# Restart zeros of a segmented scan: written by copies, or by the decays' own exponential

## The chip, the core and the metric

The kernel runs on one core of a Trainium2 chip. The metric is the device time of one execution in microseconds. The core's engines are TensorE (PE; its weight loads are PEld), VectorE (DVE), ScalarE (ACT), GpSimd (POOL) and SyncE (SP), which issues the DMAs. Each engine works through its own queue in order, and semaphores tie the queues together. "L815" is line 815 of the kernel before.

## What is computed

The input is an image batch of 8 x 256 x 48 x 48. Layer 0 is a group norm, a projection, a similarity of all 2304 tokens with each other, the 16 nearest per token, and a weighted mean of their features. Layer 1 is a group norm and two Mamba blocks in a row. What matters here is the recurrence in a Mamba block, over the tokens of an image, for each of 512 channels and 16 states:

```
dA = exp(dt[t] * A)              # A = -exp(A_log), negative
h  = h * dA + dt[t] * B[t] * x[t]
y[t] = sum over states of h * C[t]
```

A token's state is the decayed state of the token before it, plus an input. At the first token h is zero; later chunks of tokens go on from the chunk before.

## The kernel before

**Tiling.** The 2304 tokens are cut into 6 chunks of T = 384. One chunk of one block of one image is a *unit*; 8 images, 6 chunks and 2 blocks make 96 units. A unit has 16 *steps*, each with 32 channels; the 128 partitions hold those 32 channels four times, for four groups of states, so that each partition has Q = 4 states. A step falls into two *parts* of HQ = 2 states. That makes 3072 parts, and the main loop runs over them, with part m as its counter.

**A part.** `decay(m)` (L815) has ScalarE compute two rows of 384 exponentials, one for each state, from the replicated step sizes `dtr` with the decay rate as scale. They go to one of two PSUM tiles, used in turn (`decays(m)`). `make_bx` (L791) has GpSimd multiply the inputs, 4 states at a time, into `bx`. `run_scan(m)` (L830) has VectorE run one scan over both states at once, 2 x 385 elements: each state has a column ahead of its 384 tokens. In that *restart column* the decay is zero and `bx` holds the incoming state (`take_up`, L803 and L805), so the scan drops what it carried from the other state and begins from there.

**Who multiplies by C.** A table, `SHARE`, divides the parts. In 2040 parts the scan writes over `bx`, and GpSimd does the multiply (L860). In the other 1032 parts, here called *V parts*, the scan writes over the decays in PSUM, and VectorE does the multiply (L832). Afterwards the restart columns hold states in place of zeros, and since the decays' rows are only written from their second column on, ScalarE has to put the zeros back: in `carry(m)` L847 saves the last column's states for the next chunk (`h_st`; not needed in an image's last chunk), then L848 copies two zeros from a constant tile.

**Order.** It is written out by hand. Within a turn m of the loop ScalarE's queue gets `carry(m - 1)`, then `decay(m + 1)`, which writes the same PSUM tile that part m - 1 has left. VectorE's queue gets the scan of part m, with its multiply if it is a V part. Two tables, `between` and `behind`, place all other work of a unit (projections, convolution taps, normalization, loads) at fixed parts, ahead of the scan or behind it; layer 0 of the next image is spread over the same loop.

**Loads.** `load_rep` (L565) brings a step's 32 rows of step sizes (`dtr`) and of their products with x (`dtxr`) from HBM to four groups of partitions, as four DMAs of 48 KB, about every second part, into three buffers in turn.

Of the kernel before, what the change touches and what calls it, by code (L numbers as in the profile page):

```python
# [8 lines left out]
F32 = mybir.dt.float32  # L9
BF16 = mybir.dt.bfloat16  # L10
AF = mybir.ActivationFunctionType
ALU = mybir.AluOpType
# [3 lines left out]
P = 128  # L16
GSIZE = 8
TAKEN = -4.0
TINY = 1e-24
FAR = 64.0  # L20


@with_exitstack
def tile_conv_preact(
# [18 lines left out]
    nc = tc.nc  # L43
# [8 lines left out]
    T = 384  # L52
# [3 lines left out]
    G = 32  # L56
    J = P // G
    Q = NS // J
    HQ = 2
    H = DC - 1  # L60
    PARTS = Q // HQ
    STEPS = DI // G
# [6 lines left out]


    SHARE = ("GGVGGGVVGGGGGGVG", "GGGVGVVGVVVGVGVG", "VGVGVGVVGGVVGGVG")
    JR = 1
    assert N % T == 0 and N % P == 0 and T % P == 0 and NS % (J * HQ) == 0

    const = ctx.enter_context(tc.tile_pool(name="const", bufs=1))
# [12 lines left out]
    minus = const.tile([P, P], BF16, tag="minus", name="minus")  # L88
    nc.vector.tensor_scalar(minus, ident, -FAR, None, ALU.mult)
    three = const.tile([P, 1], F32, tag="three", name="three")  # L90
    nc.gpsimd.memset(three, 3.0)
    tiny = const.tile([P, 2], F32, tag="tiny", name="tiny")
    nc.gpsimd.memset(tiny[:, 0:1], -TINY)
    nc.gpsimd.memset(tiny[:, 1:2], TINY)
    ones_mean = const.tile([P, P], F32, tag="ones_mean", name="ones_mean")
# [38 lines left out]
    A_sb = const.tile([P, DEPTH, STEPS, Q], F32, tag="A_sb", name="A_sb")  # L134
# [15 lines left out]
                A_log[d].rearrange("(i g) s -> g i s", g=G)[:, :, j * Q : (j + 1) * Q],  # L150
            )
    nc.scalar.activation(A_sb, A_sb, AF.Exp)
    nc.vector.tensor_scalar(A_sb, A_sb, -1.0, None, ALU.mult)

    h_st = const.tile([P, DEPTH, STEPS, Q], F32, tag="h_st", name="h_st")
    tail = const.tile([P, DEPTH, CB, H], F32, tag="tail", name="tail")
# [1 line left out]
    def rsqrt_start(r, var, eps):  # L158

        nc.scalar.activation(r, var, AF.Ln, bias=eps)  # L160
        nc.scalar.activation(r, r, AF.Exp, scale=-0.5)

    def rsqrt_end(eng, r, var, eps, name):

        t = small.tile(list(r.shape), F32, tag="newton", name=f"nt_{name}")
        if eng is nc.gpsimd:
            v = small.tile(list(r.shape), F32, tag="newton_v", name=f"nv_{name}")
            eng.tensor_scalar(v, var, eps, -0.5, ALU.add, ALU.mult)
            eng.tensor_mul(t, r, r)
            eng.tensor_mul(t, t, v)  # L170
            eng.tensor_scalar(t, t, 1.5, None, ALU.add)
            eng.tensor_mul(r, r, t)
            return

        nc.scalar.activation(t, r, AF.Square)
        eng.scalar_tensor_tensor(var, var, eps, t, ALU.add, ALU.mult)
        eng.tensor_scalar(var, var, -0.5, 1.5, ALU.mult, ALU.add)
        eng.tensor_mul(r, var, r)
# [49 lines left out]
    def layer0(b, left, pool, ps0, alone):  # L228
# [50 lines left out]
        def inverse_norm(c):  # L279
            rn[c] = small.tile([P, TB], F32, tag="rn", name=f"rn_{b}_{c}")  # L280
            rsqrt_start(rn[c], n2[c], tiny[:, 1:2])
            rsqrt_end(nc.gpsimd, rn[c], n2[c], TINY, f"rn_{b}_{c}")

# [233 lines left out]
    with tc.tile_pool(name="first", bufs=1) as pool0, tc.tile_pool(  # L517
        name="first_ps", bufs=1, space=PSUM
# [7 lines left out]
    with tc.tile_pool(name="setup", bufs=2) as setup:  # L526
        for d in range(DEPTH):
            for t in range(DC, DC + 1):
                dg = setup.tile([P, DB, P], F32, tag="dg", name=f"dg_{d}_{t}")
                for k in range(DB):  # L530
                    f = cw[:, d, k, t : t + 1] if t < DC else dpar[:, d, k : k + 1]
# [3 lines left out]
    keep = ctx.enter_context(tc.tile_pool(name="keep", bufs=2))  # L535
# [2 lines left out]

    banks = [ps.tile([P, 1024], F32, tag=f"da{i}", name=f"da_{i}", bufs=1) for i in range(2)]
    for bank in banks:
        nc.vector.memset(bank, 0.0)

    zeros = const.tile([P, HQ], F32, tag="zeros", name="zeros")
    nc.gpsimd.memset(zeros, 0.0)

    def decays(m):
        return banks[m % 2][:, 511 - T : 513 + T]
# [8 lines left out]

    def load_rep(unit, what, ik):

        k, i0 = divmod(ik * JR, J)
        t = keep.tile([P, JR, T], F32, tag=f"{what}r", name=f"{what}r_{unit['u']}_{ik}", bufs=3)
        src = unit[f"{what}_d"][k].rearrange("(i g) t -> g i t", g=G)
        for j in range(J):
            nc.sync.dma_start(t[j * G : (j + 1) * G], src[:, i0 : i0 + JR, :])  # L565
        unit[f"{what}r"][ik] = t

    def load_bc(unit, i):
# [184 lines left out]
    def silu_z(unit):  # L753
# [3 lines left out]
        for e in range(DB - 1):  # L757
# [9 lines left out]
    units = [  # L767
        dict(at=order.index((c, d)), b=b, c=c, d=d, u=f"{b}_{c}_{d}", left=lefts[b], pe={}, xc={}, BC=[], z={}, pw={},
             dt=[], dt_d={}, dtx_d={}, dtr={}, dtxr={}, bx={}, y={}, inw={}, dmat={}, taps={}, xi={}, cv={},
             pd={})  # L770
        for b in range(B) for c, d in order
    ]
    NSTEP = len(units) * STEPS

    def at(n):

        return units[n // STEPS], n % STEPS, n % STEPS // J

    def on_pool(unit, i, p):

        stage = 2 if unit["b"] + 1 == B else 0 if TOPK[0] <= unit["at"] < TOPK[1] else 1
        return SHARE[stage][(i * PARTS + p) % BLOCK] == "G"

    def make_bx(n):


        if n >= NSTEP:
            return
        unit, i, k = at(n)
        bx = keep.tile([P, Q, 1 + T], F32, tag="bx", name=f"bx_{n}", bufs=8)  # L790
        nc.gpsimd.tensor_tensor(  # L791
            bx[:, :, 1:], unit["BC"][0],
            unit["dtxr"][i // JR][:, i % JR : i % JR + 1, :].to_broadcast([P, Q, T]), ALU.mult,
        )
        unit["bx"][i] = bx

    def take_up(n):

        if n >= NSTEP:
            return  # L800
# [6 lines left out]
    def decay(m):  # L807

        n, p = divmod(m, PARTS)
        if n >= NSTEP:  # L810
            return
        unit, i, k = at(n)
        da = decays(m)
        for s in range(HQ):
            nc.scalar.activation(  # L815
                da[:, s * (1 + T) + 1 : (s + 1) * (1 + T)], unit["dtr"][i // JR][:, i % JR, :],
                AF.Exp, scale=A_sb[:, unit["d"], i, p * HQ + s : p * HQ + s + 1],
            )

    def run_scan(m):  # L820
        n, p = divmod(m, PARTS)
        if n >= NSTEP:
            return
# [12 lines left out]

    def carry(m):


        n, p = divmod(m, PARTS)  # L840
        if not 0 <= n < NSTEP:
            return
        unit, i, k = at(n)
        if not on_pool(unit, i, p):
            h = decays(m).rearrange("p (q t) -> p q t", q=HQ)
            if unit["c"] + 1 < NCH:
                nc.scalar.copy(h_st[:, unit["d"], i, p * HQ : (p + 1) * HQ], h[:, :, T])  # L847
            nc.scalar.copy(h[:, :, 0], zeros)  # L848

    def pool_part(n):  # L850

        if not 0 <= n < NSTEP:
            return
# [47 lines left out]
    def leave(unit, cb):  # L901
# [17 lines left out]
        (-35, center), (7, in_proj, 5), (24, sum_states, 2), (-33, variance), (-21, in_proj, 0),  # L919
        (-15, taps, 1), (38, out_proj, 0), (-15, taps, 2), (-14, taps, 3), (-34, square),  # L920
        (39, leave, 0), (23, load_rep, "dt", 14), (5, load_rep, "dt", 5), (-4, load_bc, 1), (38, out_proj, 1),
        (17, load_d, 2), (-17, tap, 1), (18, load_rep, "dtx", 13), (-8, times_x, 1), (19, gate, 1),
        (-22, normal), (1, load_rep, "dt", 3), (0, load_rep, "dtx", 4), (15, load_rep, "dt", 10), (6, load_rep, "dtx", 7),
        (10, load_rep, "dtx", 9), (12, load_rep, "dtx", 10), (20, load_rep, "dtx", 14), (11, gate, 0), (-29, spread_root),
        (-19, load_in, 5), (33, load_out), (-22, load_in, 0), (21, load_rep, "dt", 13), (-20, tap, 0),
# [28 lines left out]
    for n in range(LEAD):  # L954
        make_bx(n)
    take_up(0)
    decay(0)
    other = iter(())
    begun, started = None, False
    end = max(part for part, *_ in between + behind)  # L960
    for m in range(PARTS * NSTEP - HOOKS + end + 1):
        n, p = divmod(m, PARTS)
        w, hook = divmod(m, HOOKS)
        if m % (HOOKS * len(order)) == 0:
            image = w // len(order) + 1
            other = layer0(image, lefts[image], keep, ps, False) if image < B else iter(())
            begun, started = None, False
        carry(m - 1)
        decay(m + 1)
        if p == 0:  # L970
            make_bx(n + LEAD)
            pool_part(n - 1)
            take_up(n + 1)
        else:
            carry_pool(n - 1)
        for f, unit, args in inner.get(m, ()):
            if f is load_v and unit["left"] is not units[w]["left"]:
                for _ in other:
                    pass
            f(unit, *args)  # L980
        run_scan(m)
        for f, unit, args in outer.get(m, ()):
            f(unit, *args)
        if not started:
            for _ in range(2):
                if begun is None:
                    begun = next(other, 0)
            started = begun is not None and (m + 1 - PHASE - begun) % BLOCK == 0
        else:
            next(other, None)  # L990
# [41 lines left out]
```

## Time and profile before

| | |
|---|---|
| time, median of 3 runs | 10088.27 us (10084.85 to 10095.08) |
| span of the profiled execution | 10083.0 us |
| layer 0 of the first image, alone | about the first 500 us |
| exponentials of the decays, L815 | 6144, mean 584 ns |
| scans, L830 | 2040 at 1747 ns into `bx`, 1032 at 1755 ns into `da` |
| multiply of a V part, L832 | 1032, mean 958 ns |
| save of the state, L847 | 832, mean 158 ns |
| zero copy, L848 | 1032, mean 163 ns, 168.0 us in all |
| loads of step sizes, `dtr` | 6144 of 48 KB, 1.8 us to landing in the median |

Each row is from the groups of instructions by line, or from the list of DMA issues. A group's busy time is no measure of what it costs: an engine that is ahead can do it while it would otherwise wait. The idle time ahead of a group and the name of who ended it tell where an engine is held up, and the chain of waits, followed back from the last instruction, tells which of these hold-ups passed to the end of the run.

### The profile page before, as it was taken

How to read it: one execution, taken by the hardware profiler on the slowest of the kernel's cores; microseconds unless marked ns; L12 is line 12 of the kernel's file. 1: busy time of each engine (PE TensorE's matmuls, PEld its weight loads, DVE VectorE, ACT ScalarE, POOL GpSimd, SP SyncE). 2: the span in 40 equal slices, each digit the busy share in tenths (PEclk: the TensorE clock that was granted, in tenths of full speed). 3: DMA queues.
4: the chain of work that ended last, by engine and by line, in shares of the span. 5: the costliest groups of instructions: out<-in, count | busy, mean ns of one | idle time of the engine just before them, and what ended most of it. 6: DMA issues, size and time to landing. Idle time of an engine off the chain costs nothing. (4 is left out here: it accounts for less than half of the span.)

```text
span 10083.0 us, 134837 instructions
## 1 busy us (share of the span) xinstructions
PE 8011.2 (79%) x36736; PEld 4387.2 (44%) x36736; DVE 8971.1 (89%) x7992; ACT 7487.2 (74%) x16998; POOL 8944.0 (89%) x3928
## 2 busy tenths in 40 slices
PE   8878886888868888688876888778886888866655
PEld 6544443444434444344443444344443444422222
DVE  4479998899979999799997999989998899988898
ACT  4477786778767777678776777777876778777776
POOL 0079998899989999799997999989998899999998
PEclk9989997899978999799988999889997899977777
DMA  1144444444444444444444444444445444444444
GB/s 31 34 126 122 137 128 144 118 133 124 140 132 130 124 137 129 135 125 137 124 140 128 128 129 135 131 132 126 135 127 146 119 131 128 137 133 133 140 137 121
DMA packets 1243512, 1271.44 MB, mean 126 GB/s; under 512 B 266592, under 2 KB 1215840, under 8 KB 1242752
## 3 DMA queue, kind: packets, MB, share of 16 engines
q1 hardware_dynamic: 1230496, 1262.45, 43.8%
q8 instruction: 293, 4.80, 0.2%
q14 instruction: 467, 3.83, 0.1%
q10 hardware_dynamic: 12256, 0.36, 0.1%
HBM read 1048.94 MB, written 212.86 MB: 125 GB/s over the span
## 5 line engine op out<-in xcount | busy, mean ns | idle before, releaser
L791 POOL TENSOR_TENSOR bx<-BC,dtxr 128x1536 f32<-128x1536 f32 x1536 | 5301.9, 3455 | 81.4 <-PE y L878 37.8
L815 ACT ACTIVATE da<-dtr,A_sb 128x384 f32<-128x384 f32 x6144 | 3585.8, 584 | 817.3 <-DVE bx L830 626.6
L830 DVE TENSOR_TENSOR_SCAN bx<-da,bx 128x770 f32<-128x770 f32 x2040 | 3525.2, 1747 | 191.8 <-ACT da L815 142.3
L860 POOL TENSOR_TENSOR bx<-bx,BC 128x1536 f32<-128x1536 f32 (+1 forms) x1320 | 3306.5, 2505 | 253.2 <-DVE bx L830 235.7
L830 DVE TENSOR_TENSOR_SCAN da<-da,bx 128x770 f32<-128x770 f32 x1032 | 1810.9, 1755 | 247.0 <-ACT da L815 161.8
L591 PE MATMUL pe<-vn,inw 128*128 128x384 f32 (+1 forms) x3072 | 1244.9, 539 | 406.9 <-DVE xr L913 89.9
L391 PE MATMUL psim<-pos 128*128 128x512 f32 (+1 forms) x2880 | 1377.8, 611 | 203.0 <-ACT sim L400 88.5
L457 PE MATMUL po<-feat,aT 128*128 128x256 f32 x5184 | 1358.1, 411 | 21.2 <-ACT aT L446 14.9
L878 PE MATMUL y<-bx,sel 128*32 128x384 f32 x12288 | 1232.3, 537 | 40.3 <-POOL bx L860 30.6
L457 PEld LDWEIGHTS po<-feat,aT 128*128 128x128 f32 x5184 | 1027.3, 205 | 367.0 <-issue 112.1
L832 DVE TENSOR_TENSOR bx<-da,BC 128x768 f32<-128x768 f32 x1032 | 989.1, 958 | 35.5
L591 PEld LDWEIGHTS pe<-vn,inw 128*128 128x128 f32 x3072 | 585.7, 205 | 924.0 <-issue 212.1
L391 PEld LDWEIGHTS psim<-pos 128*128 128x128 f32 x2880 | 553.4, 206 | 837.9 <-issue 464.3
L878 PEld LDWEIGHTS y<-bx,sel 128*32 128x32 f32 x12288 | 398.1, 119 | 862.7 <-issue 735.5
L691 DVE SCALAR_TENSOR_TENSOR xc<-pe,cw,xc 128x384 f32<-128x384 f32 x1152 | 696.3, 611 | 37.6 <-ACT xc L683 10.4
L721 PE MATMUL pd<-dbl,dtp_sb 16*128 16x384 f32 x768 | 417.5, 658 | 340.9 <-ACT dt L730 171.2
L847 ACT COPY h_st<-da 128x2 f32<-128x2 f32 x832 | 131.6, 158 | 589.7 <-DVE bx L832 582.7
L437 PE MATMUL pt<-ident,sim 128*128 128x128 f32 x2592 | 533.3, 288 | 43.0 <-DVE v L655 18.5
L446 ACT ACTIVATE aT<-pt 128x512 f32<-128x512 f32 (+1 forms) x720 | 387.6, 547 | 230.1 <-PE pt L438 225.8
L896 PE MATMUL pw<-z,ow 128*128 128x384 f32 x1536 | 529.5, 497 | 21.0 <-DVE v L655 7.4
L429 ACT ACTIVATE rest<-left,three 128x512 bf16<-128x512 f32 (+1 forms) x720 | 467.0, 670 | 59.8 <-DVE left L414 59.8
L875 PE MATMUL y<-xc,dmat 128*128 128x384 f32 x768 | 391.7, 597 | 148.8 <-DVE xc L691 124.6
(148 smaller groups left out, 10057.2 us busy)
## 6 DMA issues: line engine op xcount, KB each, us to landing
dtxr<-dtx_d SPq DMA_DIRECT2D x6144, 48.0 KB, 1.8
dtr<-dt_d SPq DMA_DIRECT2D x6144, 48.0 KB, 1.8
BC<-bc_d SPq DMA_DIRECT2D x768, 192.0 KB, 3.7
inw<-in_in_wT_dram SPq DMA_DIRECT2D x768, 128.0 KB, 2.3
dtx_d<-dtx SPq DMA_DIRECT2D x384, 192.0 KB, 1.9
dt_d<-dt SPq DMA_DIRECT2D x384, 192.0 KB, 2.1
ow<-in_out_wT_dram SPq DMA_DIRECT2D x96, 512.0 KB, 4.1
dmat<-diag SPq DMA_DIRECT2D x384, 64.0 KB, 2.1
```

The lines of the kernel that those rows point to most:

```text
L391: nc.tensor.matmul(pm, pos[:, k, t * P : (t + 1) * P], pos[:, k, c0 : c0 + w], start=(k == 0), stop=(k == CB - 1),)
L437: nc.tensor.transpose(pt[:, q], row["sim"][:, r], ident)
L457: nc.tensor.matmul(row["po"], aT[:, m % PT, :], feat[:, m, :], start=(m == 0), stop=(m == NB - 1))
L591: nc.tensor.matmul(pe, w[:, k], unit["vn"][:, k, lo:], start=(k == 0), stop=(k == CB - 1))
L691: nc.vector.scalar_tensor_tensor(unit["xc"][e], unit["pe"][e][:, k : k + T], cw[:, unit["d"], e, k : k + 1], unit["xc"][e], ALU.mult, ALU.add,
L791: nc.gpsimd.tensor_tensor(bx[:, :, 1:], unit["BC"][0], unit["dtxr"][i // JR][:, i % JR : i % JR + 1, :].to_broadcast([P, Q, T]), ALU.mult,)
L815: nc.scalar.activation(da[:, s * (1 + T) + 1 : (s + 1) * (1 + T)], unit["dtr"][i // JR][:, i % JR, :], AF.Exp, scale=A_sb[:, unit["d"], i, ...
L830: nc.vector.tensor_tensor_scan(h, da, g, 0.0, ALU.mult, ALU.add)
L832: nc.vector.tensor_tensor(bx[:, :, 0:T], da.rearrange("p (q t) -> p q t", q=HQ)[:, :, 1:], unit["BC"][1][:, qs], ALU.mult,)
L860: nc.gpsimd.tensor_tensor(g[:, :, 0:T], g[:, :, 1:], unit["BC"][1][:, qs], ALU.mult)
L878: nc.tensor.matmul(y[j * G : (j + 1) * G, :], sel, unit["bx"][k * J + j][:, q, 0:T], start=False, stop=True, skip_group_check=True,)
L896: nc.tensor.matmul(pw, unit["ow"][:, k, cb * P : (cb + 1) * P], unit["z"][k], start=(k == 0), stop=(k == DB - 1),)
```

## The change

The decays' exponential is to write the restart zeros itself. A column with 1e30 is put ahead of the step sizes. Since each decay rate is negative, exp(rate x 1e30) is zero, so an exponential over 385 columns writes the zero and the 384 decays in one instruction. For this the step sizes get three fixed tiles of 385 columns whose first column is set once, and the loads write the columns behind it. The smallest size of a decay rate is limited to 1e-27, so that the product always stays far below zero. The zero copies, their constant tile and the first clearing of the PSUM tiles go.

```diff
+NEVER = 1e30
+LEAST = 1e-27
...
-    nc.vector.tensor_scalar(A_sb, A_sb, -1.0, None, ALU.mult)
+    nc.vector.tensor_scalar(A_sb, A_sb, LEAST, -1.0, ALU.max, ALU.mult)
...
+    steps = [keep.tile([P, 1 + T], F32, tag=f"dtr{i}", name=f"dtr_{i}", bufs=1) for i in range(3)]
+    for t in steps:
+        nc.vector.memset(t[:, 0:1], NEVER)
     banks = [ps.tile([P, 1024], F32, tag=f"da{i}", name=f"da_{i}", bufs=1) for i in range(2)]
-    for bank in banks:
-        nc.vector.memset(bank, 0.0)
-
-    zeros = const.tile([P, HQ], F32, tag="zeros", name="zeros")
-    nc.gpsimd.memset(zeros, 0.0)
...
-        t = keep.tile([P, JR, T], F32, tag=f"{what}r", name=f"{what}r_{unit['u']}_{ik}", bufs=3)
+        if what == "dt":
+            t = steps[(unit["n"] * STEPS + ik) % len(steps)]
+            rows = t[:, 1:]
+        else:
+            t = rows = keep.tile([P, T], F32, tag="dtxr", name=f"dtxr_{unit['u']}_{ik}", bufs=3)
...
-            nc.sync.dma_start(t[j * G : (j + 1) * G], src[:, i0 : i0 + JR, :])
+            nc.sync.dma_start(rows[j * G : (j + 1) * G], src[:, i0, :])
...
-                da[:, s * (1 + T) + 1 : (s + 1) * (1 + T)], unit["dtr"][i // JR][:, i % JR, :],
+                da[:, s * (1 + T) : (s + 1) * (1 + T)], unit["dtr"][i],
...
-            nc.scalar.copy(h[:, :, 0], zeros)
```

The constant JR, which was 1, is written out of the code as well; the product of L791 reads the same elements through a view without it.

More of the change, by code (lines that the diff above doesn't have):

```diff
@@ L71, in tile_conv_preact @@
     SHARE = ("GGVGGGVVGGGGGGVG", "GGGVGVVGVVVGVGVG", "VGVGVGVVGGVVGGVG")
-    JR = 1
     assert N % T == 0 and N % P == 0 and T % P == 0 and NS % (J * HQ) == 0
@@ L559, in load_rep @@
     def load_rep(unit, what, ik):
-        k, i0 = divmod(ik * JR, J)
-        t = keep.tile([P, JR, T], F32, tag=f"{what}r", name=f"{what}r_{unit['u']}_{ik}", bufs=3)
+        k, i0 = divmod(ik, J)
+        if what == "dt":
[3 more added lines that the diff above has]
+            t = rows = keep.tile([P, T], F32, tag="dtxr", name=f"dtxr_{unit['u']}_{ik}", bufs=3)
         src = unit[f"{what}_d"][k].rearrange("(i g) t -> g i t", g=G)
         for j in range(J):
-            nc.sync.dma_start(t[j * G : (j + 1) * G], src[:, i0 : i0 + JR, :])
+            nc.sync.dma_start(rows[j * G : (j + 1) * G], src[:, i0, :])
         unit[f"{what}r"][ik] = t
@@ L772, in tile_conv_preact @@
     ]
+    for n, unit in enumerate(units):
+        unit["n"] = n
     NSTEP = len(units) * STEPS
@@ L792, in make_bx @@
             bx[:, :, 1:], unit["BC"][0],
-            unit["dtxr"][i // JR][:, i % JR : i % JR + 1, :].to_broadcast([P, Q, T]), ALU.mult,
+            unit["dtxr"][i].unsqueeze(1).to_broadcast([P, Q, T]), ALU.mult,
         )
```

## The prediction

> **What bounds the kernel now.** I read the busy shares first, then the idle time in front of the scans, then the chain of waits.
>
> The page, parts 1 and 2: totals, then busy tenths of VectorE (DVE), ScalarE (ACT) and GpSimd (POOL) in 40 slices.
>
> ```profile
> PE 8011.2 (79%) x36736; PEld 4387.2 (44%) x36736; DVE 8971.1 (89%) x7992; ACT 7487.2 (74%) x16998; POOL 8944.0 (89%) x3928
> DVE  4479998899979999799997999989998899988898
> ACT  4477786778767777678776777777876778777776
> POOL 0079998899989999799997999989998899999998
> ```
>
> From slice 3 on VectorE and GpSimd both run at 80 to 100%; in the seven windows of 1200 us from 500 to 8900 us VectorE is busy 1091 to 1101 us of each and GpSimd 1117 to 1122. ScalarE has about a quarter free. It cannot be the bound by its sum, only by being late at a particular moment.
>
> Part 5 of the page: the last figures of each line are the engine's idle time just before the group and who ended it.
>
> ```profile
> L815 ACT ACTIVATE da<-dtr,A_sb 128x384 f32<-128x384 f32 x6144 | 3585.8, 584 | 817.3 <-DVE bx L830 626.6
> L830 DVE TENSOR_TENSOR_SCAN bx<-da,bx 128x770 f32<-128x770 f32 x2040 | 3525.2, 1747 | 191.8 <-ACT da L815 142.3
> L830 DVE TENSOR_TENSOR_SCAN da<-da,bx 128x770 f32<-128x770 f32 x1032 | 1810.9, 1755 | 247.0 <-ACT da L815 161.8
> L847 ACT COPY h_st<-da 128x2 f32<-128x2 f32 x832 | 131.6, 158 | 589.7 <-DVE bx L832 582.7
> ```
>
> VectorE stands idle 142.3 + 161.8 = 304.1 us for the decays' exponentials; the list of VectorE's waits puts this at 151 + 74 = 225 waits, and nine more (6.3 us) were ended by the zero copy. That is the largest wait VectorE has, and the only one the change can reach directly.
>
> The instructions of line 848, the zero copy itself:
>
> ```profile
> L848 ACT COPY da<-zeros x1032: 142/163/171, 532.5 to 10068.9; 128x2 f32<-128x2 f32 x172
>   DVE bx L832: 190.6, 131
> ```
>
> Durations are minimum, median, maximum in ns. Its own waits, 190.6 us, are for the multiply of line 832.
>
> The timeline from 9119 us (start, length, instruction, in brackets idle time before it), rows of ScalarE and VectorE:
>
> ```profile
> 9119.34 1.77 DVE L830 TENSOR_TENSOR_SCAN da<-da,bx 128x770 f32<-128x770 f32 x1 [2.10 <-ACT da L815]
> ...
> 9120.86 0.15 ACT L847 COPY h_st<-da 128x2 f32<-128x2 f32 x1
> 9121.05 0.16 ACT L848 COPY da<-zeros 128x2 f32<-128x2 f32 x1
> 9121.14 0.96 DVE L832 TENSOR_TENSOR bx<-da,BC 128x768 f32<-128x768 f32 x1
> 9121.25 1.20 ACT L815 ACTIVATE da<-dtr,A_sb 128x384 f32<-128x384 f32 x2
> ...
> 9122.47 0.15 ACT L847 COPY h_st<-da 128x2 f32<-128x2 f32 x1
> ...
> 9122.55 3.41 DVE L830 TENSOR_TENSOR_SCAN bx<-da,bx 128x770 f32<-128x770 f32 x2 [0.45 <-ACT da L815]
> ```
>
> ScalarE has fallen behind (a table load and the normalization came before), saves the state at 9120.86, writes the zeros at 9121.05, and starts the exponentials at 9121.25: the zeros hold them up by **0.20 us**, and VectorE then waits 0.45 us for them. The chain of waits runs through just this spot:
>
> ```profile
> 9121.05 0.17 ACT da L848
> 9121.22 0.02 issue
> 9121.25 0.59 ACT da L815
> ```
>
> **What the skill says.** The Trainium skill, "PSUM — Partial Sum Buffer", section "PSUM bank collisions raise a hardware error", states that two engines must not touch one bank and quadrant at once, reads included. The trace agrees: near 5021 us the zero copy starts at 5021.04, just after the multiply of 5020.05 with its 0.96 us. So taking the zeros away frees nothing from waiting for the multiply; the state copy, or the exponential, inherits that wait. "ScalarE: Activation LUTs", section "What ACT_TABLE_LOAD costs", gives 0.833 ns per element of an activation and overlap between neighbours. This prices the added column. "DMA: Bandwidth & Descriptors", section "How a descriptor splits into AXI transactions", says that a descriptor off a 256-byte boundary needs one transaction more. No row of the trace shows rows loaded at an offset of 4 bytes.
>
> **The change, part by part.**
>
> *Zero copies removed.* 1032 copies of 0.163 us; start to start they hold up the next exponential by 0.195 us (9121.05 to 9121.25, and 9130.67 to 9130.87 in a second place). Sum on ScalarE: 1032 x 0.195 = 201 us. Most of it is hidden: ScalarE waits 626.6 us for scans before exponentials and 582.7 us for the multiply before state copies, so in those spots it has time over. What lies on the path I bound twice.
>
> First, by the waits: each of 225 + 9 = 234 waits of VectorE can shrink by one copy, 234 x 0.195 = 46 us, if a zero copy stood in ScalarE's backlog each time. If only the average share of parts has one (1032 of 3072 scans, 0.34), it is 15 us.
>
> Second, by the chain: it can be followed back to about 9000 us. From there to the end I counted 44 zero copies on it, out of the 192 which the trace has in that stretch, 23%. Over 1032 copies that is 237, and 237 x 0.195 = 46 us. This is a ceiling, for when the chain shortens the next longest takes over. I take **70% of it, 32 us**: the waits are mostly much longer than the saving (304.1 / 225 = 1.35 us mean), so they do not vanish under it, but GpSimd's 93% of each window leaves little room for VectorE to run ahead.
>
> *Waits moved.* The 190.6 us pass to the next instruction in ScalarE's queue: nothing gained or lost. Behind it stand the same two exponentials, for whom the scan waits.
>
> *A wider exponential.* 384 columns become 385 in 6144 instructions. By the page's price 0.83 ns each, 5 us in all; from the rows here at most (584 - 163) / 382 = 1.1 ns, 7 us. The exponentials are 11.5% of the chain from 9000 us on, so under 1 us of it lies on the path; I put 1 us. The value 1e30 needs no other instruction.
>
> *Step sizes at an offset of 4 bytes, in three fixed tiles.* 6144 loads of 48 KB. In rows of 1536 bytes, the split gives seven transactions in place of six if rows started on a boundary before: an estimate of 0 to 17% on what a packet takes, with no trace for it. A landing takes 1.8 us in the median, most of it not transfer; I take 0.05 us more. The chain from 9000 us on held some 17 to 19 such landings; scaled by 9583 / 1083, about 160, so 8 us if the transfer is never hidden elsewhere. Only 13.9 us of waits of the exponentials were ended by these loads, since each is issued some four scans ahead, so I take 2 us, and 0 and 8 as ends. The rotation over three buffers stays, and so does the wait of a load for the exponentials of three steps before.
>
> *At the start.* Two memsets of 0.912 us at 447 us go, three of one column come: hidden, as VectorE's first scan starts at 501.8 us. The maximum in the decay rates rides in an existing instruction. The operands of GpSimd's product describe the same elements.
>
> Sum: -32 + 1 + 2 = -29 us, **10059 us**.
>
> **The rivals.**
>
> *(A) A small gain, 10059 us, chance 0.53.* The bounds above, 15 and 46 us less about 3, span 10045 to 10076.
>
> *(B) No change, 10085 us, chance 0.20.* GpSimd becomes the next wait at once. For it: 93% busy, and a scan needs its product. Against it: GpSimd itself waits 235.7 us for scans before its second multiply, so earlier scans help it. If it absorbs 90% of 29 us, 3 us are left.
>
> *(C) A larger gain, 9990 us, chance 0.12.* ScalarE's backlog also delays GpSimd's inverse norms (113.8 us waits ended by the state copy, 80.1 and 75.4 by their own inputs) and TensorE. If half of the 201 us comes back through all of these: 10088 - 100. Against it: most zero copies sit where ScalarE waits for VectorE anyway.
>
> *(D) Slower, 10130 us, chance 0.15.* The unaligned rows. "Collectives: The Full Stack", section "Rules for kernel authors", asks for 32-byte alignment of collectives' buffers, to avoid read-modify-write; nothing in this trace shows whether it applies here. If a landing grew by 0.45 us, a quarter of 1.8, then 160 x 0.45 = 72 us are added to -29: about +43. Against it: the queues' share is 43.8%, and loads run ahead.
>
> **How the numbers follow.** The forecast is A's. Below 10068 us (0.2%) lie C and nearly all of A: 0.12 + 0.50 = 0.62, rounded to 0.64 since B too has a tail there; slower is D, 0.15; the rest, 0.21, is no change. For 8 in 10, the range takes A and B whole, half of the way towards C, 10015, and the near part of D, 10105.
>
> **What would show it.** Right: line 848 gone; exponentials at 585 ns; the state copy followed by the exponential 0.19 us later; VectorE's idle time for exponentials down from 304.1 us by some 20 to 45, and GpSimd's for scans not up. Wrong: landing of step sizes clearly above 1.8 us or more waits ended by them (D); VectorE's idle for GpSimd up by what ScalarE gave back (B); exponentials well above 586 ns, which would fail the price per element.

## The result, and the profile after

| | median | of the kernel before, 95% interval |
|---|---|---|
| before | 10089.2 us (10084.85 to 10095.08, 4 runs) | |
| changed | 10046.74 us (10040.9 to 10050.36, 4 runs) | 0.9957 (0.9940 to 0.9974) |

The change takes 42.5 us off, 0.43%; the interval spans 26 to 60 us.

Engine totals, part 1 of the changed kernel's page:

```profile
PE 8025.8 (80%) x36736; PEld 4396.2 (44%) x36736; DVE 8961.5 (89%) x7993; ACT 7334.1 (73%) x15966; POOL 8943.9 (89%) x3927
```

ScalarE has 1032 instructions and 153 us less. VectorE and GpSimd do nearly what they did before (VectorE 10 us less, GpSimd the same), in a shorter span.

Part 5 of the same page, with the idle time ahead of each group at the end. L822 was L815, L837 was L830, L865 was L860, and L853 was L847:

```profile
L822 ACT ACTIVATE da<-dtr,A_sb 128x385 f32<-128x385 f32 x6144 | 3589.7, 585 | 1079.2 <-DVE bx L837 688.6
L837 DVE TENSOR_TENSOR_SCAN bx<-da,bx 128x770 f32<-128x770 f32 x2040 | 3522.2, 1746 | 168.5 <-ACT da L822 128.3
L865 POOL TENSOR_TENSOR bx<-bx,BC 128x1536 f32<-128x1536 f32 (+1 forms) x1320 | 3314.6, 2511 | 227.1 <-DVE bx L837 211.4
L837 DVE TENSOR_TENSOR_SCAN da<-da,bx 128x770 f32<-128x770 f32 x1032 | 1809.2, 1753 | 236.5 <-ACT da L822 159.0
L853 ACT COPY h_st<-da 128x2 f32<-128x2 f32 x832 | 131.9, 159 | 604.7 <-DVE bx L839 598.6
```

The wider exponential costs 585 ns in place of 584. VectorE's idle time for exponentials is now 128.3 + 159.0 = 287.3 us, 17 less than before. GpSimd's wait for scans is 211.4 us, 24 less than in its line of before:

```profile
L860 POOL TENSOR_TENSOR bx<-bx,BC 128x1536 f32<-128x1536 f32 (+1 forms) x1320 | 3306.5, 2505 | 253.2 <-DVE bx L830 235.7
```

The state copy still waits for the multiply.

The spot that the prediction showed, in the changed kernel's timeline (start, length, instruction, idle time before it):

```profile
9092.45 0.15 ACT L853 COPY h_st<-da 128x2 f32<-128x2 f32 x1
9092.64 1.21 ACT L822 ACTIVATE da<-dtr,A_sb 128x385 f32<-128x385 f32 x2
...
9093.94 3.41 DVE L837 TENSOR_TENSOR_SCAN bx<-da,bx 128x770 f32<-128x770 f32 x2 [0.25 <-ACT da L822]
```

From the start of the save to that of the exponentials it was 0.39 us, now it is 0.19; the scan's wait went from 0.45 to 0.25 us. At this spot the whole 0.20 us of the copy reached VectorE.

The list of what ScalarE and VectorE waited for before touching the tile `da` has one entry for the multiply of a V part (us, times), first before, then in the changed kernel:

```profile
  DVE bx L832: 773.3, 554
```

```profile
  DVE bx L839: 784.2, 554
```

Before, the 773.3 us were 582.7 ahead of state copies and 190.6 ahead of zero copies. In the changed kernel 598.6 us stand ahead of state copies and the rest, 185.6 us, ahead of exponentials. The wait passed on and did not shrink.

### The profile page after: what moved, and what is told of

It reads as the page before. It is cut to its first block, busy times and chain, and to the rows that moved or that the text cites. A ratio compares the mean times of both kernels' runs of the same rounds, so it can differ in the third digit from the quotient of the medians.

```text
span 10045.6 us, 133805 instructions
## 1 busy us (share of the span) xinstructions
PE 8025.8 (80%) x36736; PEld 4396.2 (44%) x36736; DVE 8961.5 (89%) x7993; ACT 7334.1 (73%) x15966; POOL 8943.9 (89%) x3927
## 3 DMA queue, kind: packets, MB, share of 16 engines
q1 hardware_dynamic: 1230496, 1262.45, 46.1%
## 5 line engine op out<-in xcount | busy, mean ns | idle before, releaser
L822 ACT ACTIVATE da<-dtr,A_sb 128x385 f32<-128x385 f32 x6144 | 3589.7, 585 | 1079.2 <-DVE bx L837 688.6
L837 DVE TENSOR_TENSOR_SCAN bx<-da,bx 128x770 f32<-128x770 f32 x2040 | 3522.2, 1746 | 168.5 <-ACT da L822 128.3
L865 POOL TENSOR_TENSOR bx<-bx,BC 128x1536 f32<-128x1536 f32 (+1 forms) x1320 | 3314.6, 2511 | 227.1 <-DVE bx L837 211.4
L837 DVE TENSOR_TENSOR_SCAN da<-da,bx 128x770 f32<-128x770 f32 x1032 | 1809.2, 1753 | 236.5 <-ACT da L822 159.0
L853 ACT COPY h_st<-da 128x2 f32<-128x2 f32 x832 | 131.9, 159 | 604.7 <-DVE bx L839 598.6
```

What stands on the lines that cost most here:

```text
L822: nc.scalar.activation(da[:, s * (1 + T) : (s + 1) * (1 + T)], unit["dtr"][i], AF.Exp, scale=A_sb[:, unit["d"], i, p * HQ + s : p * HQ + s ...
L837: nc.vector.tensor_tensor_scan(h, da, g, 0.0, ALU.mult, ALU.add)
L865: nc.gpsimd.tensor_tensor(g[:, :, 0:T], g[:, :, 1:], unit["BC"][1][:, qs], ALU.mult)
```

## The experiments

The time of each is set against runs of the kernel before on the same chip. "Change" is the difference of the two medians.

| kernel | median us | before, us | change, us | ratio, 95% interval |
|---|---|---|---|---|
| before, zero copies taken out | 10044.37 | 10092.2 | -47.8 | 0.9953 (0.9939 to 0.9967) |
| changed, zero copies back | 10089.76 | 10092.2 | -2.4 | 1.0000 (0.9992 to 1.0008) |
| changed, rows 64 bytes in | 10041.86 | 10092.2 | -50.3 | 0.9950 (0.9938 to 0.9963) |
| before, rows 4 bytes in | 10090.84 | 10092.2 | -1.4 | 0.9997 (0.9989 to 1.0005) |
| changed, copies back in 6 parts | 10076.04 | 10091.0 | -15.0 | 0.9984 (0.9978 to 0.9991) |
| changed, copies back in the rest | 10060.0 | 10091.0 | -31.0 | 0.9970 (0.9959 to 0.9981) |
| changed, two copies behind | 10126.32 | 10091.0 | +35.3 | 1.0032 (1.0019 to 1.0045) |
| changed, two copies in front | 10107.08 | 10091.0 | +16.1 | 1.0014 (1.0008 to 1.0021) |
| before, each zero copy twice | 10175.06 | 10094.97 | +80.1 | 1.0082 (1.0069 to 1.0096) |
| changed, no saves in V parts | 10030.92 | 10094.97 | -64.1 | 0.9935 (0.9923 to 0.9948) |

The three kernels without zero copies (changed, taken out, rows 64 bytes in) lie at -42.5, -47.8 and -50.3 us; their mean, **-46.9 us**, stands below for the changed kernel when others are set against it. From their intervals I estimate that this mean is uncertain by some 9 us either way; the changed kernel itself was not run again beside the later ones.

### Is it the copies?

Take them out of the kernel before:

```diff
-            nc.scalar.copy(h[:, :, 0], zeros)
```

> The kernel before with the zero copies taken out and nothing else, so its restart columns keep states after the first V parts: the restart zeros are left out of the computation. Theory (the copies' 0.195 us in front of the exponentials is the whole gain, and the offset rows give a little back): 10035 to 10048 us, at or below the changed kernel's 10047. Rival 1 (the gain comes from the fixed tiles of the step sizes, whose loads wait less): near 10089. Rival 2 (the offset rows give back much): below 10020.

Measured: 47.8 us less, with nothing else touched. Put them back into the changed kernel, at the same place (the constant tile of zeros comes back with them; that part of the edit is left out here):

```diff
+            nc.scalar.copy(h[:, :, 0], zeros)
```

> The changed kernel with the zero copy put back where it was, behind the save of the state; it writes zeros over what are states until the exponential overwrites them anyway. Theory: the loss returns, and the rest of the change shows alone: 10089 plus 0 to 10 us for offset rows and the wider exponential. Rival 1 (fixed tiles bring the gain): stays near 10047. Rival 2 (offset rows cost much): 10110 or more.

Measured: 10089.76 us, within 0.08% of before either way. So the copies are the whole gain, as far as these intervals tell. All the rest of the change (the wider exponential, the fixed tiles, rows at an offset) adds up to -2 us, with an interval of 8 us on either side. Rival 1, the fixed tiles, falls in both.

Through which wait the copies cost time is less plain. With the copies back, VectorE's idle time ahead of scans, and GpSimd's ahead of its multiply, are:

```profile
L839 DVE TENSOR_TENSOR_SCAN bx<-da,bx 128x770 f32<-128x770 f32 x2040 | 3526.2, 1748 | 193.9 <-ACT da L824 130.4
L839 DVE TENSOR_TENSOR_SCAN da<-da,bx 128x770 f32<-128x770 f32 x1032 | 1811.0, 1755 | 247.9 <-ACT da L824 157.8
L868 POOL TENSOR_TENSOR bx<-bx,BC 128x1536 f32<-128x1536 f32 (+1 forms) x1320 | 3308.4, 2506 | 254.8 <-DVE bx L839 240.0
```

VectorE waits 130.4 + 157.8 = 288.2 us for exponentials, hardly more than the 287.3 us of the changed kernel, and yet the time is 43 us longer. The three kernels with copies and the three without compare like this (us):

| kernel | VectorE's wait for exponentials | GpSimd's wait for scans | VectorE idle in all (span less busy) |
|---|---|---|---|
| before | 304.1 | 235.7 | 1112 |
| changed, zero copies back | 288.2 | 240.0 | 1116 |
| before, rows 4 bytes in | 298.2 | 241.7 | 1118 |
| changed | 287.3 | 211.4 | 1084 |
| before, zero copies taken out | 287.3 | 208.9 | 1078 |
| changed, rows 64 bytes in | 287.4 | 208.3 | 1079 |

The last two columns part the kernels with copies clearly from those without; the first hardly does (288.2 against 287.4). So the delay reaches VectorE in part under other names: a wait's name says only what ended it.

### Do rows at an offset cost anything?

The changed kernel's page looked as if they did. The queue's packets, megabytes and share of the 16 DMA engines' span, part 3 of each page, before and in the changed kernel:

```profile
q1 hardware_dynamic: 1230496, 1262.45, 43.8%
```

```profile
q1 hardware_dynamic: 1230496, 1262.45, 46.1%
```

A landing takes 1.9 us in place of 1.8, and the exponentials' waits that these loads ended went from 13.9 to 27.9 us. Two kernels took the offset away or put it alone into the kernel before:

```diff
-    steps = [keep.tile([P, 1 + T], F32, ...
+    steps = [keep.tile([P, 16 + T], F32, ...
-            rows = t[:, 1:]
+            rows = t[:, 16:]
```

> The changed kernel with its 1e30 in column 15 of a tile of 400 columns, so that the rows of step sizes begin 64 bytes into the tile in place of 4. Theory: the DMA queue's share falls from 46.1% back to about 43.8%, loads land at 1.8 us again, and the time falls by 2 to 8 us, to 10039 to 10045. Rival 2: by 20 us or more. If the longer packets have nothing to do with the offset, the share stays at 46% and the time at 10047.

```diff
+        if what == "dt":
+            t = keep.tile([P, JR, 1 + T], F32, tag="dtr", ..., bufs=3)[:, :, 1:]
```

> The kernel before with only its rows of step sizes begun 4 bytes into the tile; zero copies and exponentials as before. Theory: DMA share near 46%, time up by 0 to 8 us, 10089 to 10097. Rival 2: above 10110. If the offset costs nothing at all, 10089 and a share of 43.8%.

The four kernels of these two sections ran on one chip. Part 3 of their pages, first the kernel before without zero copies, whose rows are not moved, then the kernel before with moved rows:

```profile
q1 hardware_dynamic: 1230496, 1262.45, 45.7%
```

```profile
q1 hardware_dynamic: 1230496, 1262.45, 45.8%
```

With rows 64 bytes in it was 46.2%. So my expectation that the share follows the offset was wrong: 45.7 and 45.8% hardly differ, and on another chip, later, the kernels with copies back in some parts, whose rows do sit 4 bytes in, show 44.4 and 44.5%. The share differs from one sitting to the next (each sitting here had its own chip, so the two can't be told apart), and the page of before came from another sitting than these four. Nor is the landing a sign of the offset: in this sitting it is 1.9 us with unmoved rows too.

```profile
dtr<-dt_d SPq DMA_DIRECT2D x6144, 48.0 KB, 1.9
```

The waits that the loads ended follow the copies and not the offset: 25.6 us with unmoved rows and no copies, 16.1 us with moved rows and copies. A small effect is left open. Share times span, which is the packets' time, is 0.7% larger with moved rows in this sitting, and 1.3% larger in the last one (45.2% of 10167.8 us with each zero copy twice, unmoved; 46.4% of 10029.2 us without saves, moved); from before to the changed kernel it was 4.9%. One profile of each kernel doesn't tell whether one per cent is the offset.

In time, offset rows alone gave -1.4 us (interval -11 to +5). Moving the changed kernel's rows to 64 bytes gave 10041.86 us. That lies in the range forecast for it, but also within the noise of 10044.37 us, the kernel of the same sitting with unmoved rows and no copies.

### Which copies count?

The chain of waits of the kernel before, followed back anew from the end of each stretch of 200 us, meets 274 of the 1032 zero copies, and 171 of them in six of the 32 parts of a unit. (The count shifts somewhat with where the stretches begin.)

```diff
+    HOT = (10, 18, 19, 22, 23, 30)
+            if m % HOOKS in HOT:
+                nc.scalar.copy(h[:, :, 0], zeros)
```

> The changed kernel with the zero copy put back in six of a unit's 32 parts only (parts 10, 18, 19, 22, 23 and 30): 396 of the 1032 copies. In the kernel before, these hold 171 of the 274 zero copies that the chain of waits meets when it is followed back anew from the end of each stretch of 200 us. Theory 1 (a copy costs where it lies on the chain): 171/274 of 46 us come back, 29 us: about 10074. Theory 2 (all copies cost the same, ScalarE's time as such counts): 396/1032 of 46, 18 us: about 10063.

Its counterpart has `not in HOT`:

> The other way round: the zero copy put back in all V parts but those six, 636 copies, of which the chain before met 103. Theory 1: 17 us come back, about 10062. Theory 2: 28 us, about 10073. The two together should give back about 46 us if neither hides the other.

Against -46.9 us, the 396 copies in the six parts bring back 31.9 us, 81 ns each; the other 636 bring back 15.9 us, 25 ns each. Sum 47.8, the whole. By each kernel's own interval that is 25 to 38 us and 6 to 28 us. Set against each other, on one chip, the kernel with the fewer copies is the slower one by 16 us; were all copies equal, it would be some 11 us faster. The six parts hold 38% of the copies, 62% of those on the chain, and 67% of the cost. Theory 1 holds: a copy of 195 ns costs about two fifths of its length where the chain goes through many of them, and about an eighth elsewhere. For each copy that the chain met it is 31.9/171 = 0.19 us and 15.9/103 = 0.15 us, near the copy's full length.

### ScalarE's time, or the place in its queue?

Two small copies that nobody needs, the second reading the first, are added to each V part's turn, by a function `beside` (its text is left out here).

```diff
         carry(m - 1)
         decay(m + 1)
+        beside(m - 1)          # behind
```

> The changed kernel with two small copies from one unused constant's columns to the next (the second reads the first, so ScalarE works them off one after the other in about 0.27 us) in each V part's turn, behind the two exponentials. They take ScalarE's time but stand in front of no exponential of that turn. If ScalarE's time as such counts: 0.27/0.195 x 46 = 64 us more, about 10110. If only the delay of this turn's exponentials counts: 10045 to 10065.

In the other kernel `beside` stands ahead of `decay`.

> The same two copies in front of the two exponentials, behind the save of the state, where the zero copy was. Both theories: about 64 us more than the changed kernel, 10110. If it comes out well below the kernel with the copies behind, the place doesn't matter as I think.

ScalarE's timeline with the copies behind, then with the copies in front:

```profile
5001.58 0.18 ACT L864 COPY aside<-aside 128x2 f32<-128x2 f32 x1
5001.78 0.19 ACT L865 COPY aside<-aside 128x2 f32<-128x2 f32 x1
5001.88 0.19 ACT L887 COPY h_st<-bx 128x4 f32<-128x4 f32 x1
```

```profile
5087.01 0.16 ACT L855 COPY h_st<-da 128x2 f32<-128x2 f32 x1 [0.64 <-DVE bx L841]
5087.07 0.20 ACT L864 COPY aside<-aside 128x2 f32<-128x2 f32 x1
5087.30 0.19 ACT L865 COPY aside<-aside 128x2 f32<-128x2 f32 x1
5087.44 1.20 ACT L824 ACTIVATE da<-dtr,A_sb 128x385 f32<-128x385 f32 x2
```

Behind, they hold up the next instruction by 0.30 us (5001.58 to 5001.88). In front, the exponentials start 0.43 us after the save in place of 0.19, so 0.24 us: the first copy overlaps the save. Times 1032 that is, as an estimate, 310 and 248 us of ScalarE. Measured against -46.9 us: 82 and 63 us. Both are **0.25 to 0.26 us per microsecond of ScalarE** (0.21 to 0.30 and 0.22 to 0.28 by the two intervals). In plain time the kernel with the copies in front is 19 us faster, the sign that I had named against my theory; the shorter hold of ScalarE accounts for it, and the place makes no difference beyond that which these runs show. I had expected as one case that copies behind would be nearly free (10045 to 10065); they were not. ScalarE works its queue off in order, and when it is behind, what it does after one pair of exponentials delays the next. VectorE's list of waits tells who felt it, three lines with the copies behind, then one of the changed kernel:

```profile
DVE z L901 <- PE y L895: 170.6, 91, 10.1
DVE da L839 <- ACT da L824: 157.6, 65, 4.5
DVE bx L839 <- ACT da L824: 135.9, 192, 3.1
```

```profile
DVE z L889 <- PE y L883: 140.2, 71, 10.0
```

(Us in total, times, longest.) The waits for exponentials are 293.5 us, little more than in the changed kernel; another 42.7 us of scans' waits were ended by an added copy, and the wait for TensorE's sums is up from 140.2 to 170.6.

### Is the price constant?

Each zero copy twice, in the kernel before:

```diff
             nc.scalar.copy(h[:, :, 0], zeros)
+            nc.scalar.copy(h[:, :, 0], zeros)
```

> The kernel before with each zero copy written twice, one right after the other: ScalarE gets another 1032 x 0.195 = 201 us. If a microsecond of ScalarE costs what the removal gave back (46/201, 0.23), and goes on doing so: 10091 + 46, about 10137. If the removal sat at a threshold, and the waits behind it are already filled: clearly more, 10160 or above. If VectorE and GpSimd were the bound and ScalarE only touched it: below 10115.

And the changed kernel without the other copy in that spot, the save of the state:

```diff
-            if unit["c"] + 1 < NCH:
-                nc.scalar.copy(h_st[...], h[:, :, T])
```

> The changed kernel without the save of the state in V parts (L853); the states carried from chunk to chunk are left out there, and the store is cleared once. ScalarE loses 832 x 0.192 = 160 us in the same spot. At 0.23 per microsecond: 37 us less, about 10010. If the gain of the zero copies was all there was to get from ScalarE and VectorE and GpSimd bound what is left: above 10035.

The price is not constant. With ScalarE's time counted from the changed kernel on (count of instructions times start-to-start time):

| ScalarE's time more, us | time more, us | price of the step |
|---|---|---|
| -160 (no saves) | -17 | 0.11 |
| 0 (changed) | 0 | |
| 201 (before) | 47 | 0.23 |
| 402 (copies twice) | 127 | 0.40 |

Each step of ScalarE's time that is taken away is worth about half of the step before it. By the intervals the three prices are 0.03 to 0.19, about 0.19 to 0.28, and 0.35 to 0.48, so that the rise at the top is clear and the fall at the bottom less so. The bottom step also takes away another instruction than the other two, the save, which waits for the multiply. I had expected 0.23 throughout, 10137 and 10010; both kernels came out slower, 10175.06 and 10030.92. The former is in the range that I had given for waits that are already filled (10160 or above), the latter short of the one for an exhausted gain (above 10035). With copies twice, GpSimd pays as well. Part 5 of that page:

```profile
L861 POOL TENSOR_TENSOR bx<-bx,BC 128x1536 f32<-128x1536 f32 (+1 forms) x1320 | 3306.1, 2505 | 319.0 <-DVE bx L830 296.0
L830 DVE TENSOR_TENSOR_SCAN da<-da,bx 128x770 f32<-128x770 f32 x1032 | 1811.3, 1755 | 279.8 <-ACT da L815 188.3
```

GpSimd's waits for scans are 296.0 us, against 235.7 before and 211.4 in the changed kernel; VectorE's wait for exponentials ahead of a V part's scan is 188.3 us, against 161.8 before. Without the saves, GpSimd's waits are only 15 us below those of the changed kernel:

```profile
L864 POOL TENSOR_TENSOR bx<-bx,BC 128x1536 f32<-128x1536 f32 (+1 forms) x1320 | 3306.9, 2505 | 210.8 <-DVE bx L838 196.5
```

Why the price bends is not shown. It would fit with other chains taking over as ScalarE comes to be on time more often, but no run here isolates those.

## Why the prediction was right, point by point

**Direction and cause: right.** The forecast was -29 us, and the changed kernel gave -42.5, inside the range. The copies alone, taken out or put back, make the whole difference, and they cost most where the chain of waits met most of them. That the loss goes through VectorE's waits for exponentials, "the only one the change can reach directly", holds at the spot shown but not for the sum: with the copies back those waits are within 1 us of the changed kernel's.

**The term that was mis-sized** is the 70% taken from the ceiling of 46 us, on the ground that the next longest chain takes over. Measured, the removal gives 47.8 us, and the mean of the three kernels without copies is 46.9: all of what was called the ceiling. A discount like it shows only at the next step, in the saves, at 0.11 us per microsecond. That the sum of 46 us was hit so closely is in part luck: it scales up the last 1083 us (44 of 192 copies, 23%). The later count over the whole run, 274 copies, would have given 274 x 0.195 = 53 us.

**The bound by waits** (15 to 46 us) took only the waits that an exponential or a zero copy ended. Between before and changed VectorE's wait for exponentials fell by 17 us, short of the 20 to 45 that were announced, and the 6.3 us that a zero copy ended are gone: 23 together, half of what was gained. Its idle time in all fell by 28 us in these two profiles, and GpSimd's wait for scans, of which the prediction said only that it would not rise, by 24. The two engines' waits can't be added up, for each feeds the other. So the upper end of that bound, 46 us, agrees with the result by number and not by its account.

**Waits moved: right.** 773.3 us before and 784.2 us after for the multiply. The Trainium skill, "PSUM — Partial Sum Buffer", section "PSUM bank collisions raise a hardware error", was the ground for it: the state copy only reads, as the multiply does, and yet the trace has it wait 598.6 us for the multiply.

**The wider exponential: right**, 585 against 584 ns. Their busy time in all is 3584.0 to 3585.8 us in the four kernels with 384 columns and 3589.0 to 3591.5 us in the eight with 385. The means differ by 5.1 us, or 0.84 ns for each exponential, so the price of 0.833 ns per element in the Trainium skill, "ScalarE: Activation LUTs", section "What ACT_TABLE_LOAD costs", agrees.

**Offset rows: put at 2 us, ends 0 and 8; they cost nothing that was measured** (-1.4 us, interval -11 to +5). The prediction named a landing clearly above 1.8 us, or more waits ended by these loads, as the signs of rival D. The 1.9 us, the 27.9 us of waits and the 46.1% of the page after would have been false signs. The page on descriptors was used beyond what it states: the Trainium skill, "DMA: Bandwidth & Descriptors", section "How a descriptor splits into AXI transactions", is about where a transaction may start to read, and counts no transaction more for its example of 96 bytes off a boundary. These loads read the same rows as before; only the place written has moved. The term's upper end was also too high: the chain from 9000 us on meets 10 landings of `dtr`, and the prediction took 17 to 19. With 10, the 8 us become about 4, and rival D's 72 us about 40.

**The rivals.** No change (B) falls: GpSimd did not absorb the gain, its own waits for VectorE fell. The larger gain (C) falls by its size, 100 us, though its thought that ScalarE's delay also reaches VectorE through other engines finds support with the copies behind, where VectorE's wait for TensorE's sums rose by 30 us. Slower (D) falls with the offset.

**A misread line.** VectorE and GpSimd are not at 80 to 100% in every slice from the third on: each has slices with a 7, between 70 and 80%.

## What to carry to other kernels

Where two engines run at 90%, a third that is only 74% busy can still have a price: here 0.23 us for each microsecond taken from it, 0.40 for each one added. Count how many of the small instructions lie on the chain of waits and multiply by the start-to-start time (0.195 us here, not the 0.163 us of the row): that gave 46 us by the last tenth of the run and 53 by the whole of it, and 47 were measured. The waits of the busiest engine, sorted by who ended them, told less: about half of the gain, and nearly all of the loss with the copies back, stood under other names. And before a difference between two profiles is laid to an edit, see whether a kernel without that edit, from the same sitting, shows it too.

## What the runs showed of the hardware that was not expected

Rows of 1536 bytes took the same time, within the intervals above, whether they were written at the start of a tile, 4 bytes into it or 64 bytes into it. The DMA queue's share for the same 1230496 packets varied from 43.8 to 46.4% over the runs: kernels with rows 4 bytes in had 44.1 to 46.4%, kernels with unmoved rows 43.8 to 45.7%, and the one with rows 64 bytes in had 46.2%. A copy of two elements, 0.15 to 0.20 us long, held up the next instruction on ScalarE by 0.20 to 0.23 us where that one worked on the same tile (9121.05 to 9121.25, 5001.58 to 5001.78, 5087.07 to 5087.30), and by only 0.06 to 0.14 us where it did not (5087.01 to 5087.07, 5001.78 to 5001.88, 5087.30 to 5087.44).
